# Queries and output units by three one-pass fp32r products of exact 12-bit halves: x turned in place, queries kept in HBM until scored, Wout late, a new order

## The chip, the cores and the metric

The kernel runs on one NeuronCore of a Trainium2 chip, as one launch. The metric is the device time of that core in microseconds (us), lower is better. TensorE (PE) does the matmuls, VectorE (DVE), ScalarE (ACT) and GpSimd (POOL) the elementwise work, and nearly all DMAs are issued from the queue of SyncE (SP).

## What is computed

Two sequences of x (2 x 2048 x 640, fp32) attend to a context of 128 tokens each. The last four context tokens (`ca`) go through an adapter: 384 of its columns, stretched to 2048 rows, attend to x itself, and the result attends to the four tokens again. The sum of both goes through Wout, and bias and x are added.

```python
query = x @ Wq                                    # 2048 x 640 per sequence
hs = mha(query, enc @ Wk, enc @ Wv)               # 8 heads of 80, 124 keys
ca_q1 = einsum('btc,th->bch', ca, Wq_ca)          # 384 x 640, then gathered to 2048 rows
ca_hs1 = mha(ca_q1[:, indices, :], x, x)          # every column attends to all 2048 rows of x
ca_hs2 = mha(ca_hs1 @ Wq, ca @ Wk_ca, ca @ Wv_ca) # 4 keys
out = (hs + ca_hs2) @ Wout + b_out + x
```

## The kernel before

**Tiling.** The 4096 rows of x are eight blocks of 512 rows (n = 0 to 7, four per sequence), and sixteen units of 256 rows (m = 0 to 15, two per block). The 640 columns are five chunks of 128 (`NCH`), four of which hold most of two heads each and the fifth what is left of all eight.

**The order is written out by hand.** Every piece of work is a task, a generator that yields `Do(engine, function, after, needs, frees, marks)`. `Desk.ORDER` (from line 75) lists 2366 task numbers; `Desk.run` (line 190) takes them one by one, checks that what the task waits for is already placed, takes its slots (PSUM banks, tiles) and issues the instructions in that order on each engine. A letter behind a number picks the engine where several are possible (a ACT, v DVE, g POOL). Each engine works through its instructions in the order written, so an instruction that waits holds up all later ones of its engine. Rooms such as `banks` (4 PSUM banks, 8 late), `xslots` (2 tiles for a turned block of x), `qslots` (3), `pTs` and `kss` are what one task must give back before another may take it.

**Start.** Block 0 of x is loaded by rows and turned by PE. Its queries (`queries`, lines 1042 to 1092, and `rest_chunk`) are plain fp32 products. In each product of fp32 operands that carries 128 columns of weights, `Desk.matmul` (line 215) splits the weights into four strips of 32 columns where PE was in a strip mode before; the trace shows each fp32 matmul as two records.

**Blocks 1 to 7.** `x_load` (line 997) brings a block by nine DMAs into one staging tile (`xz`), from which five DVE transposes make the turned block in an x slot. `queries_fast` (line 1168) computes x Wq by a scheme of sums (Strassen-Winograd): four sums of quarters of Wq (`sums_of_wq`), four of quarters of x on POOL and DVE (`sums_of_x`), then products of half chunks that go to q by a copy and are added to by DVE (`q<-q,pq`). The fifth chunk is a plain product (`plain`, line 1278), cut into two fp32r halves, sent to HBM and fetched back in another layout (`away`, `landing`, `rests`). q stays in a q slot until its block has been scored (`q_free`).

**The adapter** of sequence b (`adapter`, line 1497) needs all its four blocks: for each block six groups of scores (`s`) and six DVE maxima over them (`mx`, 48 in all), then the exponentials (`ea`), and their products with x (`acc`).

**Units.** `text_scores` (line 1770) makes the scores (`sc`) of 128 rows, `softmax` takes them through DVE, ACT and POOL, turns them on DVE (`eb`) and sends them to HBM (`kept`); `probabilities` fetches them as `pT`. `hidden` makes `ph` from `pT` and the values `vpad`. The outputs are made in two ways. Units 0, 1, 2, 3, 4, 6 and 7 (`BY_SUMS`) go through `text_out_fast` (line 2108): the sums scheme again, with four sums of quarters of Wout (`sums_of_wout`), four sums of the hidden units (`hs`), and eight additions of 320 columns into the rows of x per unit. The nine others go through `text_out` (line 2205): the hidden units are cut into an upper and a lower part by `hidden_parts` (line 2227), and `out_part` (line 2252) makes each quarter of the unit (128 rows by 320 columns) from 15 matmuls on fp32r tiles.

**The three products.** With a value v cut into v = t + l, t being v times (1 - 2^-13) written to an fp32r tile, `out_part` sums over the five chunks: t t', l (4096 l'), and (t - 4096 l)(t' - 4096 l') times a constant. Up to a factor (1 + 2^-12), which the addition into the rows of x applies, the sum of the three is the exact product. Wout's parts come from `wout_parts` (line 2013), whose tiles come free only late: it runs after the adapter of the second sequence has read its operands.

Line 221 is the matmul of `Desk.matmul`, line 236 the helper of DVE, ACT and POOL, line 246 the DMA helper: nearly all instructions carry one of these three lines, and groups are told apart by tile names.

## Time and profile before

| | us |
|---|---|
| median of 2 runs | 564.91 |
| lowest, highest | 563.97, 565.86 |
| span of the profiled execution, first to last instruction | 562.1 |

The profiled execution is another one than the two that were timed, and its span lies 2.8 us below their median. The page of the profile gives each engine's busy time, the chain of work that ended last, groups of instructions by tile, and DMA queues; the trace can be asked for the same in windows of time and for the instructions in order. Busy times are unions over instructions: since a matmul's record covers also the time in which its result leaves the array, the record of the next one begins before it ends, and a group's busy time counts that overlap once for every hand-over to another group.

### The profile page before, as it was taken

What the parts mean: (1) busy time and instruction counts of PE and PEld (TensorE: products, weight loads), DVE (VectorE), ACT (ScalarE), POOL (GpSimd) and SP (SyncE); (2) the same over time, 40 slices, a digit from 0 to 9 for tenths busy, and PEclk for the clock granted to TensorE, in tenths of its full rate; (3) what the DMA queues carried; (4) which work ended last, traced back from release to release, by engine and by line L of the source; (5) the groups of instructions that cost most, each with busy time, mean ns of one, the idle gap of its engine ahead of it and who ended that gap; (6) DMA issues with size and microseconds to landing.
All of it is one profiled execution on the core that took longest, in us unless ns stands there. A gap on an engine that the chain in (4) does not pass through costs nothing.

```text
span 562.1 us, 17332 instructions
## 1 busy us (share of the span) xinstructions
PE 549.2 (98%) x7338; PEld 337.8 (60%) x7338; DVE 402.2 (72%) x621; ACT 276.3 (49%) x752; POOL 208.1 (37%) x206
## 2 busy tenths in 40 slices
PE   9999999999999999999999999999999899999997
PEld 8563455556555655455365445455554477989796
DVE  2457999999996564589999998655735886449542
ACT  3122645445338898886524524589878432111200
POOL 7002625344424522013559364512424830441040
PEclk9999999999999999999999999999999989999999
DMA  8994759774876899446558895859865367977533
GB/s 258 244 175 121 163 123 166 163 159 142 170 199 155 183 251 180 136 160 176 177 126 247 226 232 133 255 149 254 244 172 177 74 124 215 264 215 195 160 123 129
DMA packets 151549, 101.38 MB, mean 180 GB/s; under 512 B 86476, under 2 KB 130012, under 8 KB 151472
## 3 DMA queue, kind: packets, MB, share of 16 engines
q1 hardware_dynamic: 150704, 99.88, 69.5%
q8 instruction: 58, 0.95, 0.8%
q0 software_dynamic: 768, 0.40, 0.4%
q14 instruction: 19, 0.16, 0.1%
HBM read 61.34 MB, written 38.90 MB: 178 GB/s over the span
## 4 chain that ended last, share of the span: by engine, by line
PE 82%; DVE 7%; DMA 5%; ACT 2%; issue 2%; SPq 1%; DVEq 0%; ACTq 0%
PE po L221 23%; PE pq L221 23%; PE acc L221 7%; PE sc L221 6%; PE s L221 6%; PE ph L221 5%; PE pq_first L221 3%; PE pyz L221 3%; DVE mx L236 2%; ACT p L236 1%; DMA bias<-in_L_xattn_b_out_dram 1%; PE pk L221 1%; PE unread L225 1%; ACT ea L236 1%; PE pv L221 1%
## 5 line engine op out<-in xcount | busy, mean ns | idle before, releaser
L236 DVE TENSOR_REDUCE mx<-s 128x4 f32<-128x2048 f32 x48 | 109.2, 2275 | 2.9 <-PE s L221 2.8
L236 POOL TENSOR_TENSOR p<-p,r 128x992 f32<-128x992 f32 x29 | 53.8, 1856 | 141.1 <-DVE r L236 135.0
L236 ACT ACTIVATE ea<-s 128x2048 f32<-128x2048 f32 x48 | 90.4, 1884 | 25.6 <-PE s L221 25.3
L236 ACT ACTIVATE p<-sc,m 128x124 f32<-128x124 f32 x256 | 89.5, 374 | 25.7 <-DVE m L236 25.7
L236 ACT ACTIVATION_READ_ACCUMULATOR p<-sc,m 128x1 f32 x256 | 55.5, 217 | 0.0
L221 PE MATMUL pq<-xt,wq_sb 128*32 128x256 f32 x896 | 54.3, 381 | 0.6 <-DVE q L236 0.6
L236 DVE TENSOR_REDUCE m<-sc 128x4 f32<-128x496 f32 x64 | 40.6, 662 | 13.9 <-PE sc L221 13.7
L221 PE MATMUL acc<-ea,y_sb 128*32 128x384 f32 (+2 forms) x768 | 50.1, 383 | 0.0
L221 PE MATMUL ph<-pT,vpad 128*32 128x256 f32 x768 | 45.8, 380 | 0.8 <-DMA out_dram<-x_more 0.3
L236 DVE STREAM_TRANSPOSE eb<-p 128x1024 f32<-128x1024 f32 x32 | 39.5, 1233 | 4.5 <-POOL p L236 3.3
L221 PEld LDWEIGHTS pq<-xt,wq_sb 128*32 128x32 f32 x896 | 27.5, 110 | 22.9 <-issue 5.5
L221 PEld LDWEIGHTS sc<-kmain,q 64*128 64x128 f32 x512 | 31.8, 187 | 11.6 <-issue 8.4
L221 PE MATMUL pq<-xt,wq 128*32 128x512 f32 x320 | 38.8, 595 | 0.0
L221 PE MATMUL po<-wout_sums,hs 128*32 128x320 f32 x448 | 35.4, 438 | 3.5 <-DVE x_more L236 2.9
L221 PE MATMUL sc<-kmain,q 64*128 64x124 f32 x512 | 37.5, 283 | 0.1
L221 PE MATMUL po<-wout_sb,hs 128*32 128x320 f32 (+1 forms) x452 | 36.4, 434 | 0.7 <-DVE prod L236 0.6
L221 PE MATMUL po<-wout_low,ks 128*128 128x320 f32 x204 | 35.7, 308 | 0.0
L221 PEld LDWEIGHTS ph<-pT,vpad 128*32 128x32 f32 x768 | 24.4, 110 | 18.6 <-issue 2.6
L236 POOL TENSOR_TENSOR last_rows<-last_rows,bias 128x640 f32<-128x640 f32 x10 | 17.0, 1697 | 44.7 <-DMA last_rows<-in_x_dram 44.7
L221 PE MATMUL po<-wout_top,ks 128*128 128x320 f32 x180 | 32.5, 311 | 0.0
L221 PEld LDWEIGHTS acc<-ea,y_sb 128*32 128x32 f32 x768 | 21.1, 109 | 17.3 <-issue 8.6
L221 PEld LDWEIGHTS po<-wout_low,ks 128*128 128x128 f32 x204 | 31.3, 188 | 0.0
(232 smaller groups left out, 951.4 us busy)
## 6 DMA issues: line engine op xcount, KB each, us to landing
kept<-eb SPq DMA_DIRECT2D x32, 512.0 KB
pT<-kept SPq DMA_DIRECT2D x48, 256.0 KB
landing<-away SPq DMA_DIRECT2D x60, 128.0 KB
xi<-in_x_dram SPq DMA_DIRECT2D x28, 256.0 KB
x_more<-in_x_dram SPq DMA_DIRECT2D x17, 320.0 KB
out_dram<-x_more SPq DMA_DIRECT2D x16, 320.0 KB
last_rows<-in_x_dram SPq DMA_DIRECT2D x15, 320.0 KB
out_dram<-last_rows SPq DMA_DIRECT2D x14, 320.0 KB
```

The costliest lines, as they stand in the source:

```text
L221: self.pin(self.nc.tensor.matmul(out[strip], lhsT[:, strip], rhs, **kw))
L225: self.pin(self.nc.tensor.matmul(out, zeros, zeros, start=True, stop=True))
L236: return lambda *args, **kw: self.pin(getattr(engine, what)(*args, **kw))
```

## The change

- Blocks 1 to 7: the sums scheme goes. `x_part` cuts each of a block's five chunks into `top`, `low` and `mix` (fp32r), `wq_part` cuts Wq once, and `query_chunk` makes each of the five 128-column chunks of q from 15 matmuls of 128 weights by 512 columns. q is scaled by (1 + 2^-12) as it leaves PSUM; there is no addition into q any more.
- All 16 units go through `text_out`; `text_out_fast` and the sums of Wout go.
- x is loaded straight into an x slot and turned in place, chunk by chunk. The staging tile goes; there are four x slots, and one block in work takes four of them: whole, top, low, mix.
- q of blocks 2 to 7 (`AWAY`) goes to HBM by two DMAs of 512 KB as soon as it is made, and comes back by two more before its scores.
- Wout is loaded into an x slot after the last x, and cut right then. The values go to HBM at the start and come back after the last query, the bias is loaded late, and the tiles of later stages are cut from other rooms.
- The order is a new list (2451 entries).

```diff
-    FAST, SPARE, IDLE = 1, 0, 14
-    BY_SUMS = (0, 1, 2, 3, 4, 6, 7)
+    IDLE, AWAY = 14, (2, 3, 4, 5, 6, 7)
...
-    def x_load(b, sb, after):
+    def x_load(n):
+        b, sb = blocks[n]
         op = yield Do(
-            "SP", lambda at: xrow.tile([P, 4 * H], F32, tag="xz", name=f"xi_{b}_{sb}"), after, needs=[(staging, 1)]
-        )
+            "NONE", lambda at: x_tile(at[0], f"x_{b}_{sb}", [P, NCH, 512], F32), 
+            [("x slot", n - 1)] + ([("x slot", n - 2, "mix")] if n > 2 else []),
+            needs=[(xslots, 1)], marks=[("x slot", n)],
+        )
...
+        for c in range(NCH):
             yield Do(
+                "DVE", lambda c=c: desk.v_transpose(t[:, c], t[:, c]),
+                [("xi" if c < 4 else "xi rest", n, i) for i in range(4)],
+                marks=[("xc", n, c)] + ([("x", b, sb)] if c == NCH - 1 else []),
+            )
+
+    def x_parts(n):
+        b, sb = blocks[n]
+        for kind in ("top", "low", "mix"):
+            op = yield Do(
+                "NONE", lambda s: x_tile(s[0], f"x_{kind}_{b}_{sb}", [P, NCH, 512]),
+                [("x", b, sb)] + ([("x slot", n - 1, "mix")] if n > 1 else []),
+                needs=[(xslots, 1)], marks=[("x slot", n, kind)],
+            )
...
+    def x_part(n, c):
+        whole = xt[blocks[n]][:, c]
+        part = lambda kind: xp[n, kind][:, c]
+        yield Do(EITHER, lambda: top_of(part("top"), whole), [("x slot", n, "top"), ("xc", n, c)], marks=[("x top", n, c)])
+        yield Do(
+            ADDS, lambda: minus(part("low"), whole, raw(part("top"))), [("x top", n, c), ("x slot", n, "low")],
+            marks=[("x low", n, c)],
+        )
+        yield from mixing(
+            lambda: part("mix"), lambda: part("top"), lambda: part("low"), [("x low", n, c), ("x slot", n, "mix")],
+            [("x mix", n, c)],
+        )
+
+    def mixing(mix, top, low, after, marks):
+        def first():
+            if desk.engine == "ACT":
+                desk.a_activation(mix(), raw(low()), AF.Identity, scale=UP)
+            else:
+                mixed(mix(), raw(top()), raw(low()))
+        op = yield Do(("DVE", "ACT"), first, after)
+        def second():
+            assert (op.ran == "ACT") == (desk.engine != "NONE")
+            if op.ran == "ACT":
+                minus(mix(), raw(top()), raw(mix()))
+        yield Do(("NONE", "POOL", "DVE"), second, marks=marks)
...
+    def wq_part(g):
+        whole = wq_parts["whole"][g]
+        part = lambda kind: wq_parts[kind][g]
+        yield Do(ANY, lambda: top_of(part("top"), whole), ["wq4"])
+        yield Do(ADDS, lambda: minus(part("low"), whole, raw(part("top"))), marks=[("wq low", g)])
+        yield Do(ANY, lambda: times(part("low"), UP), marks=[("wq up", g)])
+        yield Do(ADDS, lambda: minus(part("mix"), raw(part("top")), raw(part("low"))), [("wq up", g), "wq read"])
+        yield Do(ANY, lambda: times(part("mix"), ACROSS), marks=[("wq mix", g)])
+
+    def queries(n):
...
+        for kind in KINDS:
+            yield Fork(one(Do(
+                "NONE", lambda: None, [("qp", n, c, kind) for c in range(NCH)], frees=lambda kind=kind: [x_at[n, kind]],
+                marks=["last " + kind] if n + 1 == len(blocks) else [],
+            )))
...
+        away = hbm.tile([P, 4, 512], F32, tag=f"q_{n}", name=f"q_away_{n}")
+        for k in range(2):
+            yield Do(
+                "SP", lambda k=k: dma(away[:, 2 * k : 2 * k + 2], q_of[n][0][:, 2 * k : 2 * k + 2]),
+                [("qc", n, c) for c in (2 * k, 2 * k + 1)], marks=[("q away", n, k)],
+            )
...
+    def query_chunk(n, c, got):
+        wait = {"top": "low", "low": "up", "mix": "mix"}
+        pq = at = None
+        for kind in KINDS:
+            def product(s=None, kind=kind):
+                to = bank(s[0], f"pq_{n}_{c}") if s else pq
+                for i in range(NCH):
+                    matmul(
+                        to, wq_parts[kind, "of"](i, c), xp[n, kind][:, i],
+                        start=(kind == "top" and i == 0), stop=(kind == "mix" and i == NCH - 1),
                     )
+                return to
+            after = [("x " + kind, n, i) for i in range(NCH)]
...
+        def out_of():
+            to = q_of[n][0][:, c]
+            if desk.engine == "ACT":
+                desk.a_activation(to, pq, AF.Identity, scale=1.0 + DOWN)
             else:
+                desk.v_tensor_scalar(to, pq, 1.0 + DOWN, None, ALU.mult)
...
     def x_free(n):
+        reads = [("x low", n, c) for c in range(NCH)] if n else [("q read", 0), ("x read", 0, 1)]
+        yield Do("NONE", lambda: None, [("yz read", *blocks[n])] + reads, frees=lambda: [x_at[blocks[n]]])
...
-        yield from (text_out_fast if m in BY_SUMS else text_out)(m)
+        yield from text_out(m)
```

More of the change, by code (lines that the diff above doesn't have):

```diff
@@ L883, in load_wout @@
     def load_wout():
+        every = [("x slot", len(blocks) - 1, kind) for kind in ("top", "low", "mix")]
+        op = yield Do("NONE", lambda s: x_tile(s[0], "wout", [P, 4, H], F32), every, needs=[(xslots, 1)])
+        most, at = op.value, op.slots[0][0]
+        rest = const.tile([P, H], F32, tag="wq4", name="wout_rest")
+        wout_in.extend([*four_rows(most), rest])
         by_head = Wout.rearrange("(c j d) n -> j d c n", c=4, j=2)
@@ new lines, in parts_of_wq, with room @@
+    def parts_of_wq():
+        yield Do("NONE", lambda: None, ["wq4"])
+        def room(kind):
+            t = const.tile([P, NCH, NCH, P], F32R, tag=f"w {kind}", name=f"wq_{kind}")
+            wq_parts[kind] = [t[:, :4, i] for i in range(NCH)] + [t[:, 4]]
+            wq_parts[kind, "of"] = lambda i, c: t[:, c, i]
+        room("top")
+        room("low")
+        pairs = wq_sb.rearrange("p n (g d) -> p n g d", g=4)[:, :, :, VR : VR + P]
+        wq_parts["whole"] = [pairs[:, i] for i in range(NCH)] + [wq4]
+        for g in range(NCH + 1):
+            yield Fork(wq_part(g))
+        yield Do(
+            "NONE", lambda: room("mix"),
+            [("wq low", g) for g in range(NCH + 1)] + ["wq turned", ("q read", 0), ("x read", 0, 1)], marks=["wq read"],
+        )
@@ L2042, in wout_parts, with parts_of_wout, room, wout_part @@
+    def parts_of_wout():
+        yield Do("NONE", lambda: None, ["last query"])
+        def room(kind):
+            t = const.tile([P, NCH, H], F32R, tag=f"w {kind}", name=f"wout_{kind}")
+            w_parts[kind] = [t[:, c] for c in range(NCH)]
+        for kind in ("top", "low", "mix"):
+            room(kind)
+        for c in range(NCH):
             yield Fork(wout_part(c))
+    def wout_part(c):
+        whole = wout_in[c]
+        part = lambda kind: w_parts[kind][c]
         yield Do(
-            "NONE", lambda: tops.append(const.tile([P, H], F32R, tag="wq4", name="wout_top_4")), ["last query"]
-        )
@@ L2322 @@
         if n:
[L2323 to L2324 removed]
+            begin(x_load(n))
         begin(yz_block(b, sb))
         if n:
[L2327 removed]
+            begin(x_parts(n))
+            begin(queries(n))
+    for n in range(len(blocks)):
+        begin(x_free(n))
     begin(adapter(0))
```

924 lines of the change are left out of this document (337 added, 587 removed), and 3 rows, old and new, of the table ORDER.

## The prediction

> **What bounds the kernel now.** I read the page first (engines, queues, the chain that ended last), then busy time in windows, then PE's instructions in order.
>
> ```profile
> span 562.1 us, 17332 instructions
> PE 549.2 (98%) x7338; PEld 337.8 (60%) x7338; DVE 402.2 (72%) x621; ACT 276.3 (49%) x752; POOL 208.1 (37%) x206
> q1 hardware_dynamic: 150704, 99.88, 69.5%
> PE 82%; DVE 7%; DMA 5%; ACT 2%; issue 2%; SPq 1%; DVEq 0%; ACTq 0%
> ```
>
> PE is busy for 98% of the span and carries 82% of the chain; DVE, the next, has 28% of idle time. So PE's work sets the time as long as the others can feed it. Windows (length, then busy us and instructions of PE, weight loads, DVE, ACT, POOL; then PE's clock, the DMA engines' busy share, GB/s) tell whether they can, stage by stage:
>
> ```profile
> 0.00:60.00 60.00, 58.07 (x552) 36.91 (x556) 30.73 (x93) 16.40 (x37) 14.99 (x57) 1.00 0.79 197
> 60.00:300.00 240.00, 238.64 (x3594) 128.57 (x3589) 198.02 (x261) 146.71 (x431) 96.44 (x78) 1.00 0.72 167
> 300.00:456.00 156.00, 150.75 (x2274) 80.61 (x2274) 114.17 (x164) 99.70 (x246) 74.50 (x59) 0.99 0.71 194
> 456.00:562.00 106.00, 101.76 (x936) 91.66 (x928) 59.23 (x106) 13.54 (x38) 22.17 (x14) 1.00 0.65 182
> 60.00:160.00 100.00, 95.50 (x113) 1.00 0.74 160
> ```
>
> The last line is DVE alone: between 60 and 160 us it was busy for 95.5 of 100 us, and PE still never ran dry. The two groups that the change touches, in windows of their own (PE only), first `pq` (queries), then `po` (outputs, by sums until 456.6, by three products after it):
>
> ```profile
> 60.00:300.00 240.00, 149.99 (x2248) 1.00 0.72 167
> 300.00:456.60 156.60, 75.50 (x990) 0.99 0.71 193
> 456.60:562.00 105.40, 80.03 (x544) 1.00 0.65 183
> ```
>
> **Term 1: queries of blocks 1 to 7.** They hold PE for at most 150.0 us, a number that counts the overlap at each hand-over. Counted from runs of one shape: 252 products of 256 columns and 35 of 512 (eight records each: two per product, times four strips).
>
> ```profile
> 242.10 1.91 PE L221 MATMUL pq<-x_sums,wq_sb 128*32 128x256 f32 x32
> 243.94 0.51 PE L221 MATMUL s<-cop,zop 32*128 32x256 f32 x8
> ...
> 246.13 1.90 PE L221 MATMUL pq<-xt,wq 128*32 128x512 f32 x16
> 247.96 0.33 PE L221 MATMUL s<-cop,zop 32*128 32x128 f32 x4
> ```
>
> From start to the next group's start, four products of 256 columns take 1.84 us, two of 512 take 1.83: 252 x 0.46 + 35 x 0.915 = 148. Longer runs pay fewer hand-overs, so I take 146. After: 7 blocks x 5 chunks x 15 = 525 matmuls of 512 columns, one record each. No row shows that shape. The nearest is the same product at 320 columns:
>
> ```profile
> 540.41 0.89 PE L221 MATMUL po<-wout_top,ks 128*128 128x320 f32 x5
> ...
> 542.59 0.89 PE L221 MATMUL po<-wout_top,ks 128*128 128x320 f32 x5
> ...
> 12.76 3.60 PE L221 MATMUL pq_first<-xt,wq_sb 128*128 128x512 f32 x8
> 16.20 0.38 PE L229 MATMUL pt_ctx<-ident,ctx_sb 128*128 128x128 f32 x2
> ```
>
> Between 540.41 and 542.59 lie the 15 matmuls of one quarter: 2.18 us, 0.1455 each. In proportion to columns 512 would take 0.233 us, the upper end. The lower end is half of an fp32 record of the same shape: eight take 3.44 us, so a half is 0.215. I take 0.228, near the end that comes from the same kind of product: 525 x 0.228 = 119.7 us (113 to 122). The term is 146 - 119.7 = -26.3 us (-24 to -37).
>
> The Trainium skill ("TensorE: Matmul & The Clock Gate", Back-to-back issue gap) gives N / 2.4 + 2.5 ns for a warm matmul, 215.7 ns at 512 columns. By that the 525 would take 113.2 us and the term would be -32.8. At 320 columns the same rule gives 135.8 ns where this trace has 145.5, so the trace does not agree there, and it ranks as a rival.
>
> **Term 2: outputs.** Seven units by sums took at most 75.5 us. By count they are 126 products of 320 columns (18 a unit):
>
> ```profile
> 349.19 2.34 PE L221 MATMUL po<-wout_sums,hs 128*32 128x320 f32 x32
> 351.35 1.26 PE L221 MATMUL po<-wout_sb,hs 128*32 128x320 f32 x16
> ```
>
> Four in 2.16 us, 0.54 each, 68 us at the least; with hand-overs 72.5. By three products a unit is 4 x 2.18 = 8.7 us, seven 61.2. The term is -11.3 us (-7 to -14).
>
> **Term 3: a wait that goes.** At 446 to 456 us the outputs sat behind the cutting of Wout on DVE and POOL; Wout is now cut some 150 us before its first use.
>
> ```profile
> 449.82 1.66 PE L221 MATMUL po<-wout_sums,hs 128*32 128x320 f32 x16 [2.85 <-DVE x_more L236]
> 440.00:480.00 40.00, 36.66 (x430) 26.33 (x427) 32.86 (x54) 14.98 (x39) 16.20 (x13) 0.96 0.57 140
> ```
>
> The wait of 2.85 us goes, and so does the clock's dip to 0.96 over 40 us, worth 1.6: -4.5 us (0 to -4.5).
>
> **Term 4: new waits.** The cutting of x is the new work on the path: five chunks a block, each a `top`, a `low` and a `mix`; Wq once, six groups of five steps; seven more units of hidden parts. Prices from rows of the same operations:
>
> ```profile
> L236 ACT ACTIVATE ks<-ph 128x512 fp32r<-128x512 f32 x11 | 6.4, 589 | 33.8 <-PE ph L221 33.8
> L236 POOL TENSOR_TENSOR x_sums<-xt 128x512 f32<-128x512 f32 x12 | 15.4, 1283 | 1.8 <-ACT rests L236 1.8
> L236 DVE SCALAR_TENSOR_TENSOR ks<-ks 128x512 fp32r<-128x512 f32 x5 | 3.7, 748 | 0.1
> L236 DVE TENSOR_TENSOR ks<-ph,ks 128x512 fp32r<-128x512 f32 x18 | 12.1, 684 | 2.0 <-ACT ks L236 1.6
> L236 DVE TENSOR_TENSOR q<-q,pq 128x512 f32<-128x512 f32 x28 | 18.6, 672 | 4.6 <-PE pq L221 4.5
> L236 DVE TENSOR_REDUCE mx<-s 128x4 f32<-128x2048 f32 x48 | 109.2, 2275 | 2.9 <-PE s L221 2.8
> ```
>
> A block costs ACT 5 x 0.589 for the tops, POOL 5 x 1.28 for the lows and DVE 5 x 0.75 for the mixes, 3 to 6.4 us an engine beside 17 us of its own products: hidden in sum. DVE's balance: the additions into q go (-18.6), half of the additions into the output rows (28 of some 0.47, -13) and the sums (about -10); mixes of x come (in the new order 35 mixes of all are sent to ACT, 21 of them in the first half, so 14 x 0.75 = 10.5, and some seconds and lows, 10), and hidden parts of seven units (lows 7 x 2.5 x 0.684 = 12, mixes about 10). It ends near 405 to 430 us, under PE's 510 or so. But by stages it is tighter. Until the last query, PE has 59 us of start, 120 of queries and about 80 of adapter, `pyz` and scores, 260 us; DVE has the start (31), all 48 maxima (109, a few in the start), turns, shuffles and parts, about 245, or 94%. Before, 95.5% was carried with PE dry for nothing, so cover exists; it is gone where a block changes: PE can't take block n+1 until the slot of `top` n is given back, and then one top and the lows stand before it. Wholly uncovered that is 0.59 + 5 x 0.69 = 4 us a change, 28 us in all; wholly covered 0. Before, the same kind of chain (x turned, two sums on POOL) was covered but for 1.4 us between 60 and 300. I take 12 us, under half of the upper end, because the cover (DVE) is fuller.
>
> **Moved at no cost, and what covers it.** q of six blocks goes out and back, 24 DMAs of 512 KB on SP's queue; x, values and Wout are moved DMAs. An engine that waits for q back is PE in `sc`, queued behind it all later PE work; the order puts it blocks later. If that cover is gone, see the DMA rival. Turning in place costs the same five transposes.
>
> **Sum:** 562.1 - 26.3 - 11.3 - 4.5 + 12 = 532.0 us of span; the median shown lies 2.8 above the profiled span, so 535.
>
> **Rivals.**
>
> (a) *The page's price, and full cover.* One-pass matmuls at the lower end (-32.8) and no new wait: 562.1 - 32.8 - 11.3 - 4.5 + 2.8 = 516. Against it stands the row of 320 columns. 0.08.
>
> (b) *DMA becomes the bound of the middle stage.* Load now is 0.695 x 562.1 = 391 us for 99.9 MB.
>
> ```profile
> kept<-eb SPq DMA_DIRECT2D x32, 512.0 KB
> landing<-away SPq DMA_DIRECT2D x60, 128.0 KB
> ```
>
> 12.6 MB of queries add 49 us at that rate, and the later scores push about five units' `kept` and `landing` (1.5 MB each, 30 us) into the stage behind the last query. If 55 us of it lands in 200 us that are 0.71 full, the share is 0.98; at 0.9 and above I charge the excess, 19 us: 554. For it: the queue's share; against: stages of 0.79 ran without PE idle. 0.14.
>
> (c) *The four x slots make blocks serial* (the other side). A load starts only when the lows of the block before are done.
>
> ```profile
> 82.12 0.64 SPq L246 DMA_DIRECT2D xi<-in_x_dram  x1
> 100.21 3.04 DVE L236 STREAM_TRANSPOSE xt<-xi 128x512 f32<-128x512 f32 x5
> ```
>
> From the first issue of block 3's load to its turning 18 us passed. With five turns behind maxima (6.5), a top and five lows on POOL (7), and two softmax shares there before them (3.7), a block cycles in 35 us; my sum has 29 (200 us for seven). Then 7 x 6 = 42 more: 577, slower by 2%. It decides from a cycle of 35 us on; at 29 or less it costs nothing. 0.07.
>
> (d) *DVE is the bound until the last query*, because its two-input work slows beside POOL's:
>
> ```profile
> L236 DVE TENSOR_TENSOR wout_low<-wout_sb,wout_top x4: 812/1372/2192, 439.7 to 443.0; 128x640 fp32r<-128x640 f32 x4
> ```
>
> The same subtraction took 0.81 to 2.19 us. If some 40 new ones double in such a way (0.7 more each, 28 us) and DVE has 15 to spare, 13 to 28 us come on top: 555 to 563, say 558. 0.11. The Trainium skill ("SBUF — State Buffer", Who interferes with whom) says that a two-input DVE operation from SBUF contends with GpSimd's reads over an exclusively held port; the spread of that row agrees.
>
> **Chances.** Forecast 535 (its own range 519 to 547): 0.60; (a) 0.08, (b) 0.14, (c) 0.07, (d) 0.11. A measurement here tells about 2%: faster is below 553.6, slower above 576.2. Faster: 0.60 + 0.08 + half of (b) and a third of (d) + what of the rest falls short, 0.80; slower: most of (c), 0.06; same 0.14. The range 518 to 557 leaves out half of (a), (c) and half of (d), under 0.2.
>
> **What would show it.** Right: `pq` as records of 128 x 512 with about 0.228 us from start to start, `po` of all units in quarters of 2.18 us, PE above 95% busy, no row of an idle PE above some 3 us. (a) shows as 0.216; (b) as `sc` or `ph` waiting for `q` or `pT` DMAs, with slices of DMA at 9; (c) as `pq` or `pyz` waiting for transposes or x DMAs once a block; (d) as DVE at 97% or more to the last query, with `mx` late. The forecast is wrong if PE is idle for more than 30 us or if a matmul of 512 columns takes over 0.25.

## The result, and the profile after

| | before | after |
|---|---|---|
| median of 2 runs, us | 564.91 | 626.03 |
| lowest, highest | 563.97, 565.86 | 625.74, 626.32 |
| span of the profiled execution | 562.1 | 624.6 |

The changed kernel is slower by a ratio of 1.106 (95% interval 1.096 to 1.116). The forecast was 535 us with a range of 518 to 557: wrong in sign.

The page of the profile after, in the same lines that were shown of before, and PE's granted clock in 40 slices, which before was 9 in all slices but one of 8:

```profile
span 624.6 us, 12817 instructions
PE 561.7 (90%) x4991; PEld 406.8 (65%) x4991; DVE 422.2 (68%) x641; ACT 297.9 (48%) x794; POOL 243.7 (39%) x225
PEclk9999897899999999999959897979889799999999
q1 hardware_dynamic: 154672, 113.99, 71.3%
PE 44%; DVE 18%; DMA 15%; issue 8%; ACT 6%; POOL 5%; SPq 3%; DVEq 0%; ACTq 0%; POOLq 0%
```

No engine is full. PE falls from 98% to 90%, at a clock that dips in ten places, and its share of the chain that ended last from 82% to 44%; what PE lost went to DVE, DMA and others: a kernel that was bound by one engine now waits from hand to hand.

Two things make PE's 561.7 us look larger than they are: overlapping records, and records stretched by the slower clock. The next table is worked out from PE's records in order. A record counts up to the start of the next one, the rest is idle, and half of the work's time under a half clock counts as lost. Maxima and exponentials are counted by their starts. The stages are cut at the first score of the adapter, at the last query, at the last exponential of the adapter and at the end of PE's work.

| stage | length | PE idle | lost to the clock | work at full clock | maxima | exponentials |
|---|---|---|---|---|---|---|
| before, to the last query | 45.3 to 295.4: 250.1 | 1.9 | 0.0 | 248.2 | 34 | 24 |
| before, to the last exponential | to 435.9: 140.6 | 2.2 | 0.0 | 138.4 | 14 | 24 |
| before, to the end | to 558.1: 122.1 | 3.6 | 1.5 | 117.0 | 0 | 0 |
| after, to the last query | 51.3 to 310.4: 259.1 | 24.3 | 5.9 | 228.9 | 48 | 24 |
| after, to the last exponential | to 421.3: 110.8 | 14.7 | 13.0 | 83.2 | 0 | 24 |
| after, to the end | to 620.8: 199.5 | 18.4 | 7.0 | 174.1 | 0 | 0 |

Over the whole span idle time rose from 7.7 to 57.9 us (+50.2), lost clock from 1.5 to 25.9 (+24.4), and work fell from 547.8 to 535.9 (-11.9). These sum to +62.7, by which the end of PE's work moved (558.1 to 620.8); the span grew by 62.5.

The same stages as the windows of the trace have them (length, then PE, weight loads, DVE, ACT, POOL, clock, DMA share, GB/s), two of before and three of after:

```profile
45.30:295.40 250.10, 248.19 (x3730) 132.93 (x3726) 204.79 (x272) 150.38 (x444) 93.99 (x78) 1.00 0.70 164
295.40:435.90 140.50, 138.33 (x2093) 74.14 (x2097) 100.89 (x143) 91.44 (x232) 62.95 (x48) 1.00 0.75 209
```

```profile
51.30:310.40 259.10, 234.79 (x1783) 145.92 (x1782) 209.39 (x238) 150.68 (x345) 119.58 (x100) 0.97 0.66 158
310.40:421.30 110.90, 96.19 (x1139) 68.64 (x1138) 66.83 (x100) 82.92 (x216) 46.67 (x27) 0.86 0.75 210
421.30:624.60 203.30, 181.03 (x1706) 159.93 (x1702) 120.25 (x216) 50.78 (x208) 46.98 (x35) 0.95 0.74 196
```

In the first stage DVE is busy for 209 of 259 us, about as before, and PE has 19 us less work than before and yet takes 9 us longer. In the second, PE is idle although outputs are what it lacks: they begin at 346.1 (304.7 before). The third holds nearly all of them and its share of waits.

PE's waits in the whole of the changed kernel (total, times, longest):

```profile
PE ph L220 <- DMA pT<-kept: 9.1, 2, 8.0
PE s L220 <- DVE mx L235: 9.0, 11, 2.6
PE s L220 <- ACT ea L235: 8.2, 11, 2.0
PE pq L220 <- POOL wq_mix L235: 6.7, 1, 6.7
PE ph L220 <- DMA pT<-p: 4.8, 2, 3.7
PE ph L220 <- DMA landing<-away: 4.6, 1, 4.6
```

There is no wait for `q_back`, and none for a transposed x. The largest single waits are data that arrive late (`pT`, `landing`) and one part of Wq (`wq_mix`); the most frequent are the adapter's scores, which wait for the maximum or the exponential before them. Up to the last query these scores account for 12.1 of the 24.3 us of idle time (9.0 for maxima, 3.1 for exponentials), `wq_mix` for 6.7.

The wait of 6.7 us at 90 us has a cause far from where it shows. The chain, in order of time (start, length, what):

```profile
81.20 1.16 DVE eb L235
...
82.38 0.51 SPq L245
...
83.02 9.75 DMA v<-vpad
...
92.85 0.73 ACT zop L235
...
93.65 1.28 POOL zop L235
...
95.00 1.82 POOL wq_mix L235
...
96.86 4.01 PE pq L220 x10
```

The values, which the change sends to HBM at the start, were queued on SP behind a `kept` that waited for DVE; the transfer then took 9.75 us. Its tile was what ACT's `zop` waited for, POOL's `zop` stood behind that, POOL's last part of Wq behind that, and PE behind all.

### The profile page after: what moved, and what is told of

Its sections match the earlier page's. It is cut to its first block, busy times and chain, and to the rows that moved or that the text cites. A ratio compares the mean times of both kernels' runs of the same rounds, so it can differ in the third digit from the quotient of the medians.

```text
span 624.6 us, 12817 instructions
## 1 busy us (share of the span) xinstructions
PE 561.7 (90%) x4991; PEld 406.8 (65%) x4991; DVE 422.2 (68%) x641; ACT 297.9 (48%) x794; POOL 243.7 (39%) x225
## 4 chain that ended last, share of the span: by engine, by line
PE 44%; DVE 18%; DMA 15%; issue 8%; ACT 6%; POOL 5%; SPq 3%; DVEq 0%; ACTq 0%; POOLq 0%
PE pq L220 13%; PE po L220 9%; DVE mx L235 5%; PE s L220 5%; PE ph L220 4%; PE acc L220 4%; DMA kept<-eb 3%; DVE ks L235 3%; ACT ea L235 3%; SPq L245 3%; DMA landing<-away 2%; PE pq_first L220 2%; PE pyz L220 2%; PE sc L220 2%; ACT p L235 2%
## 5 line engine op out<-in xcount | busy, mean ns | idle before, releaser
L235 DVE TENSOR_REDUCE mx<-s 128x4 f32<-128x2048 f32 x48 | 109.6, 2283 | 11.7 <-PE s L220 10.6
L235 ACT ACTIVATE ea<-s 128x2048 f32<-128x2048 f32 x48 | 90.4, 1883 | 29.2 <-PE s L220 28.9
L235 POOL TENSOR_TENSOR p<-p,r 128x992 f32<-128x992 f32 x21 | 39.8, 1894 | 77.2 <-DVE r L235 77.2
L220 PE MATMUL ph<-pT,values 128*32 128x256 f32 x768 | 52.0, 423 | 19.0 <-DMA pT<-kept 9.1
L220 PE MATMUL pq<-x_mix,wq_mix 128*128 128x512 f32 x175 | 48.6, 416 | 6.8 <-POOL wq_mix L235 6.7
L220 PEld LDWEIGHTS ph<-pT,values 128*32 128x32 f32 x768 | 28.8, 121 | 37.6 <-issue 24.9
L220 PE MATMUL pq<-x_top,wq_top 128*128 128x512 f32 x175 | 48.7, 413 | 1.0 <-DVE halves L235 1.0
L235 DVE TENSOR_REDUCE m<-sc 128x4 f32<-128x496 f32 x64 | 40.6, 661 | 11.5 <-PE sc L220 11.5
L220 PE MATMUL pq<-x_low,wq_low 128*128 128x512 f32 x175 | 47.0, 405 | 0.0
L235 POOL TENSOR_TENSOR x_low<-x,x_top 128x512 fp32r<-128x512 f32 x29 | 36.2, 1279 | 22.4 <-PE pq L220 18.7
L220 PEld LDWEIGHTS pq<-x_mix,wq_mix 128*128 128x128 f32 x175 | 32.4, 194 | 18.8 <-POOL wq_mix L235 7.2
L220 PEld LDWEIGHTS pq<-x_top,wq_top 128*128 128x128 f32 x175 | 31.9, 193 | 15.2 <-issue 4.1
L220 PEld LDWEIGHTS po<-wout_top,ks 128*128 128x128 f32 x228 | 36.1, 195 | 5.0 <-issue 1.6
L220 PE MATMUL sc<-kmain,q_back 64*128 64x124 f32 x384 | 32.5, 296 | 6.9 <-DVE ks L235 3.4
L220 PEld LDWEIGHTS pq<-x_low,wq_low 128*128 128x128 f32 x175 | 31.4, 188 | 10.6 <-issue 4.5
```

Of the source, the lines that this page charges most:

```text
L220: self.pin(self.nc.tensor.matmul(out[strip], lhsT[:, strip], rhs, **kw))
L235: return lambda *args, **kw: self.pin(getattr(engine, what)(*args, **kw))
```

## The experiments

Times of single runs, in us; the kernel before, run beside them on the same chip, took 564.7 to 568.3. "Last query" is the end of the last `pq`.

### The order

The same instructions in another order on every engine, laid by a timing model with the durations of the trace. Every entry keeps its engine; the numbers differ because tasks are numbered as they begin. Entries 250 to 261 of the list, counted from 0:

```diff
-    19 178 52 200 210 199 159 201 212 180 211 206
+    14 159 159 200 200 200 200 208 201 159 18 210
```

> The changed kernel with the same instructions, tiles and transfers, but each engine's list laid in another order: one worked out from the durations and landing times of the profile after, so that what is late does not stand ahead of what is ready. Theory 'order' (the 58 us in which PE stands idle and the half clock behind it come from the order of the in-order queues, not from the new products): 565 to 590 us, PE idle under 30 us, granted clock above 0.975. Theory 'transfers' (the 12.6 MB of queries that go out and back load the DMA engines until probabilities and rests land late, in any order): idle after 320 us stays above 25 us, 600 us or more. Theory 'arithmetic' (the one-pass products cost as much as what they replace): 615 us or more whatever the order.

601.21 us, below what the theory of arithmetic asks for and above the range of the theory of order: idle time fell to 39.8 us, not under 30. The theory of transfers has the time, but not the idle time after 320 us, which is 11.9. PE's waits now:

```profile
PE s L220 <- DVE mx L235: 11.7, 13, 2.4
PE s L220 <- DVE cop L235: 6.4, 2, 5.9
PE s L220 <- ACT ea L235: 4.9, 10, 1.4
PE ph L220 <- DMA pT<-p: 4.3, 2, 3.9
```

The waits for `kept`, `landing` and `wq_mix` are gone. By stages: 258.1, 99.3 and 183.6 us long, against 259.1, 110.8 and 199.5. The order was worth 25 us, 16 of them in the last stage, where idle time fell from 18.4 to 5.2 and lost clock from 7.0 to 1.7. The first stage did not move: last query at 312.8.

A second list, with landing times and the clock's dips in the model:

```diff
-    19 178 52 200 210 199 159 201 212 180 211 206
+    52 219 20 223v 159 183 222 18 223 220 221 222
```

> The changed kernel once more with the same instructions in another order, now worked out with the landing times of the first re-laid run and with the clock as the traces show it (a stretch of 3.4 us in which PE is busy under about 0.63 is followed by half clock). Theory 'order': what was left of the waits goes on falling, 578 to 592 us, PE idle under 32 us, granted clock above 0.975. Rival 'the rest is not order' (a buffer, an engine or the transfers hold what is left): 597 us or more.

603.80 us, last query at 313.7, on the rival's side. A third list, with a second tile for the turned probabilities (`eb`) and the values' transfers cut at partition 112:

```diff
+    WIDE = slice(0, 112), slice(112, NK)
...
-            frees=[(yzs, 0)],
+            frees=[(yzs, 0)] if (b, sb) != blocks[-1] else [], grows=[(ebs, 1)] if (b, sb) == blocks[-1] else [],
...
-                "SP", lambda b=b: dma(kept[b, :NK], vpad[b][:NK].rearrange("p h d -> p (h d)")),
+                "SP", lambda b=b: [dma(kept[b, r], vpad[b][r].rearrange("p h d -> p (h d)")) for r in WIDE],
```

> As the run beside it (re-laid with the clock), and two more edits: a second buffer for the turned probabilities from the last y rows on (in the place of the yz tile, free by then), and the four transfers of the values cut at partition 112 (in the profile after, the whole ones of 124 partitions land in 9 to 10 us with 4 landing records, others of 256 KB with 16 records in 2 to 5 us). If the buffer and the slow values still hold the order back: 4 to 10 us under the run beside it. If a good order hides both: within 3 us of it.

603.77 us, last query at 315.2: neither edit shows in the time. As a control, the kernel before went through the same model:

```diff
-    18 176a 164 36 164g 161 16 36 18 18 167g 171
+    17 166 165 18 18 18 18 36 16 117 17 176
```

> Control: the kernel before, its instructions laid in an order from the same timing model. PE's work in its profile is 547.8 us at full clock and PE stands idle for 7.7 us, so an order can hardly give more than 8 us. Theory 'the order of the changed kernel is poor and that of the kernel before good': 555 to 572 us. Rival 'any order of such a kernel can be improved by 25 us': 540 us or less, which the profile's PE work excludes unless that work shrinks too.

575.28 us, 9 us slower than its own order. So the model doesn't improve just any order, and the new order left at least its 25 us lying. Three lists that agree within 3 us still end some 35 us above the kernel before: what is left wasn't found by moving instructions with this model.

### The transfers

The two transfers of the values moved forward in SP's queue, ahead of the `kept` that waited:

```diff
-    19 178 52 200 210 199 159 201 212 180
+    19 178 52 12 12 200 210 199 159 201
...
-    216 180 216 216 12 21 217 217
+    216 180 216 216 21 217 217 221
```

> The changed kernel with one thing moved: the two transfers that take the values out (372 KB each) are issued on SP ahead of the y rows and of the first kept probabilities instead of behind them. In the profile after, the first is issued at 83.0 us, lands at 92.8, and the z operand, then the mixed part of Wq, then PE wait for it. Theory 'order': the 6.7 us of PE idle at 90 us and the 6.8 us at half clock behind it go, 614 to 620 us. Rival (the x of the next block is late anyway, so that PE waits a few us further on): the idle moves on, 622 to 628 us.

620.89 us. The wait at 90 us went, a smaller one came (3.7 us for `x_low` at 72 us), and the last query came 6.2 us earlier: that chain cost about 5 us of the whole.

Query traffic cut to a quarter of its bytes:

```diff
-                "SP", lambda k=k: dma(away[:, 2 * k : 2 * k + 2], q_of[n][0][:, 2 * k : 2 * k + 2]),
+                "SP", lambda k=k: dma(away[:, 2 * k : 2 * k + 2, :P], q_of[n][0][:, 2 * k : 2 * k + 2, :P]),
...
-                part = slice(st % 4 * P, (st % 4 + 1) * P)
+                part = slice(0, P) if n in AWAY else slice(st % 4 * P, (st % 4 + 1) * P)
```

> The changed kernel with a quarter of the query traffic: of blocks 2 to 7 only the first 128 tokens' queries go out and come back, and the scores of all four tiles of such a block are taken from them, so three quarters of that traffic (9.4 MB) are left out; the number of transfers and the order stay. Theory 'transfers': the 18.5 us that PE waits for probabilities and rests after 400 us fall below 6, and the time to 595 us or less. Theory 'order': those waits hang on what stands ahead on SP, DVE and POOL, not on bytes; 612 us or more.

615.66 us: 9.4 MB less traffic is worth 10 us, none of it before the last query (310.2) and 7 of it between there and the last exponential. Of the waits, `landing` fell, but `pT` did not:

```profile
PE ph L220 <- DMA pT<-kept: 11.4, 2, 7.2
PE ph L220 <- DMA pT<-p: 3.6, 2, 2.7
PE ph L220 <- DMA landing<-away: 1.4, 1, 1.4
```

### The clock

Products of no use that keep PE busy where `ph` waits longest:

```diff
-                return hidden(m, c0, n, bank(s[0], f"ph_{m}_{c0}"))
+                ph = bank(s[0], f"ph_{m}_{c0}")
+                for _ in range({8: 44, 5: 24, 12: 20}.get(m, 0) if c0 == 0 else 0):
+                    desk.warm(ph[:, :P], ident)
+                return hidden(m, c0, n, ph)
```

> The changed kernel with 44, 24 and 20 matmuls of the identity (128 columns, into the bank that the next product overwrites) ahead of the hidden products of units 8, 5 and 12, where PE stood idle for 8.0, 4.6 and 3.7 us for their probabilities. If the half clock (10.2, 6.8 and 3.4 us behind those three waits) comes from PE standing idle: these windows go, the waits are filled, and the time is 8 to 10 us shorter, 615 to 619 us. If the clock is set by something else: windows at the same places, 625 to 630 us.

631.89 us. Here is the wait at 446 us in the changed kernel, and below it two of the same windows with the filler (after the window and its length comes PE's busy time; the clock is the third number from the end):

```profile
444.50:447.90 3.40, 1.35 (x10) 1.09 (x8) 1.02 (x1) 0.00 (x0) 0.00 (x0) 1.00 0.92 208
447.90:451.30 3.40, 0.00 (x0) 0.00 (x0) 0.00 (x0) 0.62 (x1) 0.00 (x0) 0.54 1.06 236
451.30:454.80 3.50, 0.99 (x12) 0.63 (x16) 0.00 (x0) 0.00 (x0) 0.00 (x0) 0.50 1.07 299
```

```profile
447.90:451.30 3.40, 3.40 (x26) 3.40 (x25) 1.54 (x2) 0.00 (x0) 1.85 (x1) 1.00 0.95 245
451.30:454.80 3.50, 3.50 (x34) 3.50 (x33) 0.00 (x0) 0.62 (x1) 0.00 (x0) 1.00 1.02 226
```

The clock stays full, so its dip does follow from the idle time. In the last stage the 88 fillers added 19.7 us of work (0.224 each) and took away 14.2 us of idle time and 5.3 us of lost clock: an even exchange. The second stage came out 3.6 us longer, for which no cause was sought. Filling a wait gains nothing here; the waits are what has to go.

### The first stage

Which of four things holds the last query near 310 us: PE's products, the cutting of x, the x slots, or the adapter's maxima? First PE alone, relieved of 140 of its 525 query matmuls:

```diff
-                for i in range(NCH):
+                for i in range(NCH) if kind != "mix" else (NCH - 1,):
```

> The changed kernel in its own order, with 140 of the 525 query matmuls left out: of each chunk's mixed product only the last of five is made, so all waits stay and the queries of blocks 1 to 7 are wrong. At 0.232 us each that is 32.5 us of PE work. If PE's work sets the pace up to the last query (theory 'arithmetic'): 28 us less or more, 598 us or below. If waits set it (theory 'order'): the time falls by 15 us or less, 611 us or more, and PE's idle time grows by what the time does not fall.

629.69 us, last query at 312.9: 33.5 us less work for PE gained nothing. It became 19.2 us of idle time and 17.7 us of lost clock; what it would have gained at full clock isn't separated.

Next the cutting and the slots. The changed kernel's trace spoke strongly for the slots: blocks 4, 5 and 7 begin their tops within 0.3 us of the last `top` product of the block before (154.6 and 154.9, 195.8 and 195.9, 273.1 and 273.2), block 3 within 0.1 us of its last `low` product, and the blocks' products follow each other every 35.7 us, (282.8 - 68.4) / 6, just where the prediction's rival of serial blocks begins. Two kernels with the same 385 query matmuls, without most of the mixes of x and without Wq's mix, the slots held in one and eased in the other:

```diff
-            [("x mix", n, c)],
+            [("x mix", n, c)], c == NCH - 1,
...
+            if not made:
+                return
...
-                        to, wq_parts[kind, "of"](i, c), xp[n, kind][:, i],
+                        to, wq_parts["low" if kind == "mix" else kind, "of"](i, c), xp[n, kind][:, i],
```

> The changed kernel with part of its work left out: of each block's mix only the fifth chunk is made, the mixed product is one matmul of five and takes its weights from the low part of Wq, and Wq's mix isn't made. The x slots are taken and given back as before, the mix tile with them. It is compared with the kernel that left the 140 matmuls out and kept the work on DVE, ACT and POOL (629.7 us, last query 312.5). Theory (the chain of x slots sets the pace up to the last query: a block's tops wait for the last product of the block before): little changes, 618 to 632 us, last query at 300 to 313. Rival E (the cutting of x on DVE, ACT and POOL sets it): with 28 of 35 mixes gone the last query is at 295 or before and the time at 612 or less. Rival O (the order in which each engine stands sets it): 622 to 632, last query after 305.

```diff
+        if i == 4:
+            t = const.tile([P, NCH * H], kind, tag="w mix", name=name)
+            return t[:, : NCH * 512].rearrange("p (c n) -> p c n", c=NCH)
...
-                needs=[(xslots, 1)], marks=[("x slot", n, kind)],
+                needs=[(xslots, 1)] if kind != "mix" else [], marks=[("x slot", n, kind)],
...
-["wq turned", ("q read", 0), ("x read", 0, 1)], marks=["wq read"],
+["wq turned", ("q read", 0), ("x read", 0, 1)], marks=["wq read"], frees=[(xslots, 4)],
```

> The same part left out, and the same matmuls as in the run above; but the mix takes no x slot (none is made; the one matmul of the mixed product takes a row of Wq's low part instead), and the room of Wq's mix, which is free here, is a fifth x slot. So five slots serve whole, top and low, and no tops wait for the products of the block just before. Theory (slots): the last query comes at 290 or before, 15 us or more before that of the run with the slots held, the wait of the second block's tops near 86 to 94 us goes, and the time falls by 12 us or more. Rival E: within 6 us of the run with the slots held, which itself has fallen. Rival O: within 6 us of it as well, and both stand near 625.

628.99 and 629.11 us, last query at 311.4 and 311.7. The slot theory falls, for this order. With the fifth slot the tops of block 7 were made from 263.7 on, 9.5 us earlier than in the changed kernel, but their products began at 282.5, where they had begun before (282.8). The tops of blocks 4 and 5, which start at a coincidence too, moved by 0.2 and 1.2 us only (155.1 and 194.7): they now start right behind the transposes of x that stand before them on DVE. The coincidence in time was real, and nothing on the path was shown to hang on it. What PE and DVE did wait for in this kernel, from the first score to the last query (PE's waits, then DVE's):

```profile
PE s L223 <- DVE mx L238: 29.4, 19, 8.7
PE s L223 <- ACT ea L238: 5.9, 9, 1.3
```

```profile
DVE mx L238 <- PE s L223: 20.2, 20, 3.0
DVE q L238 <- PE pq L223: 7.7, 2, 5.2
```

Each waits for the other: scores for the maximum before them, the maximum for its scores. So the maxima were shortened, in the changed kernel and in the three above:

```diff
-                        lambda q4=op.value: desk.v_tensor_reduce(mx[:, ct, u, :, sb], q4, AX.X, ALU.max),
+                        lambda q4=op.value: desk.v_tensor_reduce(mx[:, ct, u, :, sb], q4[:, :, :256], AX.X, ALU.max),
```

> The changed kernel, but each of the adapter's 48 maxima is taken over half of its columns (the other half is left out of the maximum, which only shifts the exponentials): a DVE instruction of some 1.2 us in place of 2.28. Theory Q (the one set of four PSUM banks for the adapter's scores sets the pace up to the last query: it is held by scores and then by a maximum or an exponential, 219 of the 259 us between the first score and the last query): 48 x 1.1 = 52 us of holding go, the last query comes at 285 to 300 (310.4 before), the time falls to 598 to 616. Rival V (DVE's own work sets it): the same fall, since DVE has the same 52 us less. Rival O (the written order of each engine, whoever is ready): last query after 304, time 617 to 627.

> The same cut of the maxima in the kernel that leaves 140 query matmuls and the mixes of x out and has the fifth slot (629.1 us, last query 311.3), where PE, the cutting and the slots have all been relieved. Theory Q: with the passes shorter as well the last query comes at 280 or before, and the time at 605 or less. Rival V: the same. Rival O: last query after 304.

> Half of the columns of each maximum left out, in the kernel that leaves out 140 query matmuls and nothing else (629.7 us, last query 312.9). With the maxima halved alone the last query came at 303.4, with matmuls, cutting and slots relieved as well at 287.6. Theory P (the pair that sets the first stage is PE's matmuls and the maxima): 286 to 294, 606 to 613 us. Theory S (it is the x slots and the maxima) and theory C (it is the cutting of x and the maxima): 299 to 305, 617 to 624 us.

> The same half maxima in the kernel that leaves out 140 query matmuls and 28 of the 35 mixes of x with the slots held as before (629.0 us, last query 311). Theory P: as the run above, 286 to 294. Theory C: 286 to 294 where the run above stays at 299 to 305. Theory S: 299 to 305 here too, and only the fifth slot brings 287.6.

All eight in one table (time and last query):

| left out or eased | maxima whole | maxima halved |
|---|---|---|
| nothing else | 626.03, 310.4 | 621.70, 303.4 |
| 140 query matmuls | 629.69, 312.9 | 612.80, 296.4 |
| and 28 of 35 mixes of x, and Wq's mix | 628.99, 311.4 | 612.94, 294.5 |
| and the slots, and the other 7 mixes | 629.11, 311.7 | 607.37, 287.6 |

In the left column nothing gains. With the maxima halved the same steps bring 7, 2 and 7 us to the last query (single runs, so the 2 us say little). So the maxima come first in this stage, and the rest stands close behind: halved alone, they gain 7 us, and PE's work is then 228 of the 252 us of the stage; with everything else eased, they gain 24 of the 51 us that they were shortened by. No rival as it was put (one other resource besides the maxima) holds; the three share it. One thing is mixed in: before the last query the three lower runs of the left column lose 22.9, 25.5 and 24.0 us to the clock, the changed kernel 5.9, and the three lower ones of the right column 13.3, 12.9 and 8.6. How much of the missing gain in the left column is due to this half clock was not tried.

What about the maxima is it, DVE's time or the one set of four PSUM banks that scores, maxima and exponentials pass through? Two sets of two banks, whole maxima in two instructions each:

```diff
-                        q4 = ps_quad["later"].tile([P, 4, 512], F32, tag="sq", name=f"s1_{b}_{sb}_{ct}_{u}")
+                        q2 = [ps_quad["later"].tile([P, 2, 512], F32, tag=f"sq{h}", name=f"s1_{b}_{sb}_{ct}_{u}_{h}") for h in range(2)]
...
-                    lambda q4=q4, e=e: desk.a_activation(e, q4, AF.Exp, scale=SCALE),
+                    lambda q2=q2, e=e: [
+                        desk.a_activation(e[:, 2 * h : 2 * h + 2], q2[h], AF.Exp, scale=SCALE) for h in range(2)
+                    ],
```

> The changed kernel whole, but the set of four banks is two sets of two: each pass makes its four matmuls into the two sets, and one maximum or exponential of 1024 columns reads each, so that the scores of the next pass can go into the first set while DVE or ACT still reads the second. DVE has more to do, 48 more instructions with their fixed cost, 5 us or so. Theory Q: 0.2 to 0.4 us less for each of the 72 passes up to the last query, which comes 5 to 20 us earlier, at 290 to 305; time 603 to 620. Rival V: the last query is not earlier, 309 to 318; time 625 to 635. Rival O: within 4 us of 626.

> The same two sets of two banks in the kernel that leaves 140 query matmuls and the mixes of x out and has the fifth slot (629.1 us, last query 311.3). Theory Q: last query at 303 or before, 8 us or more earlier. Rival V: 309 to 318. Rival O: within 3 us of 311.

634.62 us in the whole kernel and 628.61 in the eased one, last query at 310.8 and 309.6: the theory of the bank set falls, as far as this way of splitting tests it (PE, in order, now waits inside each pair of products, and DVE has more to do: 96 maxima of 1.22 us, 7 us on top). That leaves DVE's own time and its place in the written order. Halved maxima in the re-laid order:

```diff
-    19 178 52 200 210 199 159 201 212 180 211 206
+    14 159 159 200 200 200 200 208 201 159 18 210
...
-                        lambda q4=op.value: desk.v_tensor_reduce(mx[:, ct, u, :, sb], q4, AX.X, ALU.max),
+                        lambda q4=op.value: desk.v_tensor_reduce(mx[:, ct, u, :, sb], q4[:, :, :256], AX.X, ALU.max),
```

> The re-laid order (601.2 us, last query 312.8) with half of the columns of each maximum left out. If the maxima on DVE hold the stage up to the last query as soon as the order does not (theory V): last query at 300 or before, time 585 to 594. If PE's own work and the order hold it (rival): last query after 305, time 596 to 602.

596.67 us, last query at 304.1: 4.5 us, less than the theory asked for. PE's work, 228.6 of the 248.5 us of its stage, is the nearest other bound here as well. The traces show one more thing: before the last query the changed kernel places all 48 maxima, the kernel before placed 34, as the busy time of `mx` on DVE shows (first before, then after; the counts hold one more short reduction for each sequence, which joins its maxima).

```profile
45.30:295.40 250.10, 77.59 (x35) 1.00 0.70 164
295.40:435.90 140.50, 32.05 (x15) 1.00 0.75 209
```

```profile
51.30:310.40 259.10, 110.11 (x50) 0.97 0.66 158
```

32.5 us of DVE's longest work moved into the very stage that was to become shorter. An order with the last maxima behind the last query was not tried.

### The second stage

Less of Wout to cut after the last query:

```diff
-        yield Do(ADDS, lambda: minus(part("low"), whole, raw(part("top"))), marks=[("wout low", c)])
-        yield Do(ANY, lambda: times(part("low"), UP), marks=[("wout up", c)])
+        yield Do(ADDS, lambda: None, marks=[("wout low", c)])
+        yield Do(ANY, lambda: None, marks=[("wout up", c)])
```

> The changed kernel, but of Wout only the top part is cut; the 20 instructions that make its low and mixed parts are left out, and the low and mixed products take the top part as weights (same matmuls). Theory W (after the last query at 310 us PE stands because Wout is cut only then, 28 us of it on POOL between 308 and 346): the first output product comes at 332 or before (346.1 with the cut), the 27.7 us of idle time and lost clock between the last query and the last exponential falls by 8 or more, time 604 to 618. Rival O (the written order and the exponentials' passes hold PE there): first output product after 338, time within 6 us of 626.

630.88 us, the first output at 348.3, and 17.6 us idle in place of 14.7. POOL's busy time in the stage fell by more than half, to 21.37 us, for nothing: PE now waited 5.0 us at 325 us for the values' DMA, and stood as before for exponentials. That the cut of Wout holds the outputs back falls, for this order. The chain to the first output shows what both kernels share, the values on their way back (here the changed kernel; start, length, what):

```profile
319.23 10.18 DMA values<-v
...
329.65 1.07 PE ph L220 x16
```

The first `ph` starts when they have landed, 10.2 us after their issue, and with the cheaper Wout it starts at 330.04, behind the same transfer of 10.16 us. It is not the only hold: in the third list, where both pieces of the first such transfer landed within 3.5 us, the chain passes over the exponentials, and the first output came at 350.7.

No kernel of these beats the one before. The best that computes everything is the re-laid one at 601.21; PE's work at full clock, 538 us there, leaves 27 us below 565 for all idle time, all lost clock and the start and end of the kernel without PE.

## Why the prediction was wrong

- **Term 1, queries (-26.3): mis-sized, -11.5 measured.** Work before 145.9 us, as forecast (146); after 134.4 instead of 119.7. The step that failed is 525 x 0.228. Groups of PE in order of time:

```profile
173.40 1.43 PE L220 MATMUL pq<-x_top,wq_top 128*128 128x512 f32 x5
174.76 0.51 PE L220 MATMUL s<-cop,zop 32*128 32x384 f32 x8
175.20 1.07 PE L220 MATMUL acc<-ea,y_sb 128*32 128x128 f32 x16
176.20 1.43 PE L220 MATMUL pq<-x_mix,wq_mix 128*128 128x512 f32 x5
```

  Five products hold PE for 1.36 us, 0.272 each. The chain has 2.50 us for ten and 3.67 for fifteen, so five more cost 1.14 to 1.17, 0.228 to 0.234 each: the price was right, and the 0.2 us that a stretch of them costs between products of another kind was left out. Half of it lies at either end: from start to start the first matmul takes 0.34 us, those within 0.23, the last up to the next product 0.33. The trace has 60 stretches, half of them of five: 60 x 0.2 + 525 x 0.231 = 133 us, close to the 134.4 measured. The forecast took its price from a row of fifteen, where the queries mostly run in fives and tens between scores and `acc`. The rule of the Trainium skill ("TensorE: Matmul & The Clock Gate", Back-to-back issue gap), about 216 ns at 512 columns, does not agree with the 228 to 234 ns measured here. Rival (a), which takes the lower price, ended further off.

- **Term 2, outputs (-11.3): -6.4 measured**, 150.9 to 144.5 us of work for all units. The quarter was right (2.18 forecast; 538.77 to 540.98, 2.21, below); the seven units by sums held 69.6 us (150.9 less 9/16 of 144.5), not 72.5, and the new seven 63.2, not 61.2.

```profile
538.77 0.90 PE L220 MATMUL po<-wout_top,ks 128*128 128x320 f32 x5
539.50 0.89 PE L220 MATMUL po<-wout_low,ks 128*128 128x320 f32 x5
540.24 0.90 PE L220 MATMUL po<-wout_mix,ks 128*128 128x320 f32 x5
540.98 0.89 PE L220 MATMUL po<-wout_top,ks 128*128 128x320 f32 x5
```

- **Not in the sum:** `sc` and `acc` rose by 3.3 and 3.2 us of work, though their products are the same. Terms 1 and 2, these and small ones make -11.9 in place of -37.6.

- **Term 3 (-4.5): the old wait went, its reason did not hold.** No row of PE waits for the cutting of Wout. But Wout is not cut some 150 us before its first use: the cutting runs from 303.3 to 344.5 us and the first output begins at 346.1. Without the low and mixed parts it began no earlier (348.3), so this cost nothing here. The outputs moved to where other data are late, and the gain was lost many times over in the last stage.

- **Term 4 (+12, bounds 0 to 28): the step that failed and decided.** Idle time and lost clock rose by 74.6 us: 28 up to the last query, 25 from there to the last exponential, 20 behind it. The bounds held one mechanism, the change of a block, and that was not what PE waited for; and they put nothing on the later stages. In the first stage the step that misled was DVE's balance, "about 245, or 94%" of 260 us, with the conclusion that cover exists. DVE's amount was near enough (235 us to the last query, 209 of them from the first score on), but PE's 229 us and DVE's 209 in that stage do not lie side by side as two sums: scores and maxima alternate, 48 times, and wait for each other in part (the scores 9.0 us in 11 waits, the maxima 10.6 us in 13). The last query came at 310 us where the sum had it at 260: 32 of these 50 us are idle time and lost clock, and 19 are PE's own work (278.6 us up to there), 15 of them the queries of term 1.

- **"Moved at no cost"** failed in two places. q itself was never waited for, as said. The values, named among what is moved, cost about 5 us at 90 us through a tile, ACT and POOL; and three quarters of the bytes of q cost 10 us. That is the side of the DMA rival, which was priced at 19 and given 0.14, but its sign shows only in part: without them `landing` falls from 4.6 to 1.4 us and `pT` does not. What stood ahead of the values in SP's queue wasn't named.

- **The new order** was not priced at all. It left 25 us, 16 of them after the last exponential: outputs begin 41 us later than before, and most of their work (123.6 of 144.5 us) come in a stage where PE waits for `pT` and `landing`.

- **Rivals.** Serial blocks (577, 0.07) had the cycle right, 35.7 us, and the cause wrong, as far as the fifth slot tests it. DVE as the bound (558, 0.11; its lower end is 535 + 13 = 548, not 555) had the engine right. Its mechanism is there, but small: of the fourteen mixes on DVE the four that ran beside POOL for half of their time or more took 1.13 to 1.60 us, the ten others 0.65 to 0.69. Two of six lows were slowed as well (2.35 and 0.86 us, alone 0.67 to 0.68). That is 4 to 5 us in all, where 13 to 28 were counted:

```profile
L235 DVE SCALAR_TENSOR_TENSOR x_mix<-x_low,x_top x14: 651/685/1601, 68.7 to 260.3; 128x512 fp32r<-128x512 f32 x14
L235 DVE TENSOR_TENSOR x_low<-x,x_top x6: 671/682/2347, 162.9 to 250.6; 128x512 fp32r<-128x512 f32 x6
```

- **What would show it:** of the signs named, both for being wrong came true: PE was idle for 57.9 us (30 was the limit), and 134.4 us for 525 matmuls are 0.256 us each, hand-overs included (0.25).

Of the 92.6 us between the forecast span of 532.0 and 624.6, PE's work accounts for 25.7 (37.6 less 11.9), the clock for about 26 and idle time for about 41. By the runs, the order holds 25 us and the bytes of q 10 (the two overlap, and weren't run together). In the first stage the maxima are shown to come first, by halving them; whether through DVE's time, its written order or the hand-over to the scores is not shown. With them eased and everything else too, 37.5 us of idle time and lost clock remain there (28.9 and 8.6), and whether the 14 maxima that moved ahead of the last query explain them stays open. So do the second stage's 27.7 us: re-laid orders left 16 to 24 of them, and a cheaper Wout did not lower them (30.0).

## What to carry to other kernels

Add up PE's work by groups as they will stand in the order, not by the price in a long row: here 0.2 us a stretch took a third of the expected gain. When one engine is 98% busy, taking work from it pays only until the next hand-over chain; look for pairs of engines that answer each other (a score and its maximum) and count the pairs per stage, before and after the change. A resource whose release coincides with the start of what follows need not be its cause; give it a spare and see.

## What the runs showed of the hardware

**The clock drops after short waits too.** After 311.6 us PE stood for 1.31 and 1.97 us, never long in one piece:

```profile
311.60:315.00 3.40, 1.84 (x32) 1.51 (x30) 2.88 (x3) 1.66 (x5) 3.32 (x3) 1.00 0.83 217
315.00:318.40 3.40, 1.69 (x16) 0.90 (x20) 0.99 (x1) 1.66 (x1) 3.32 (x3) 0.51 0.88 225
318.40:321.80 3.40, 2.03 (x16) 1.03 (x10) 3.40 (x5) 1.87 (x9) 3.40 (x3) 0.50 0.86 199
321.80:325.20 3.40, 3.40 (x34) 2.95 (x36) 3.12 (x7) 2.77 (x9) 2.82 (x3) 0.50 0.89 259
325.20:328.70 3.50, 3.33 (x36) 1.55 (x37) 3.22 (x4) 3.19 (x6) 3.42 (x2) 0.50 0.54 165
```

A stretch of 3.4 us with PE busy for 1.84 us was followed by four at half clock, 13.7 us. On the grid of 3.413 us on which the clock changes, ten stretches of the changed kernel at full clock were followed by half clock, the fullest with PE busy for 0.635 of it, and the least busy that stayed at full clock had 0.644. In the three re-laid kernels stretches of 0.51 to 0.64 stayed full as well, and one of 0.73 was followed by half clock, so this is no sharp rule. The Trainium skill ("TensorE: Matmul & The Clock Gate", Part 1: The HAM clock gate) has the window, 3413 ns, and an idle window as the condition; these rows show that a half-busy one can suffice.

**A transfer over 124 partitions was slow.** The values, 372 KB, took 9.75 us at 83 us and left four landing records where other transfers leave sixteen. The Trainium skill ("DMA: Bandwidth & Descriptors", Why a DMA increments its semaphore by 16 and not by 1) says that the number of engines is the largest up to 16 that divides the outer size of both sides, which is 4 for 124; the trace agrees with the four. The third list, which cuts the same transfers at partition 112, bears this out: its first piece of 112 partitions (336 KB), issued at 86.4 us, left sixteen records, the last 3.6 us after the issue.
